# Graph layer and masked attention on one core: the last batch's output projection by head pairs, with its own copy of the weights, two queues for the last rows, and new step lists for the first and last turns

## The chip, the cores and the metric

The kernel runs on one core of one Trainium2 chip. The metric is the device time in microseconds (us): the median of the runs shown is 2990.31 us (2990.01 to 2992.61, three runs). All durations below come from one profiled execution of the kernel before, which took 2989.65 us. Its span, from the first to the last recorded event, is 2987.9 us, so 1.75 us lie around it.

## What is computed

There are 64 batches of 256 tokens with 512 features, all in fp32. For each batch the reference does two layers:

```python
deg = sum(adj, -1); agg = (adj @ x) / max(deg, EPS)
x = layernorm(x + relu(concat([x, agg]) @ W.T))          # layer 0
q, k, v = x @ Wq.T + bq, x @ Wk.T + bk, x @ Wv.T + bv     # 8 heads of 64
s = (q @ k.T) * SCALE * (adj + adj)                        # per head
x = layernorm(x + softmax(s) @ v @ Wo.T + bo)              # layer 1
```

## The kernel before, in words

All matrix products run on TensorE (PE in the profile) in fp32. One product of 128 rows by 512 columns is one instruction in the code and shows as two in the trace; the trace's "x4" is therefore two instructions.

**Steps.** The work of a batch is cut into some 215 named steps, each a few instructions on one engine (or a group of transfers). A step's name and its batch are listed by hand in three strings: START (the batches up to the first full turn, absolute batch numbers), PLAN (one turn of two batches, repeated) and END (counted back from the last batch: `:1` is batch 63, `:2` is batch 62). The engines take their instructions in exactly this order, each engine in order for itself; semaphores put in by the framework make an instruction wait for what it reads or overwrites. So the lists decide, on each of the five queues (PE, VectorE = DVE, ScalarE = ACT, GpSimd = POOL, SyncE = SP), what stands behind a waiting instruction.

**The steps that matter here.**
- `Dzx`, `Dza`, `Dadj`, `Dx`: loads of a batch's x and adj, most as four transfers each, issued by SP. `W0h0`, `W0h1`, `Wq`, `Wv`, `Wo`, `Wb`: loads of the weights and biases (Wo is one transfer of 1024 KB, Wv four of 256 KB). The built program gives the transfers eight semaphores in turn, so an issue waits until the transfer eight places before it has landed.
- `xT0`, `xT1`, `aT`, `x1T` (L401, L772, DVE): 32-by-32 transposes. `xS` (L436), `Ls` (L573), `aS`, `bS`, `yS`, `cS` (POOL): sums for the products, which are done by the Winograd form of Strassen's scheme: seven products P, L, Y, Q, V or O (numbers 1 to 7) in place of eight, gathered in three accumulators a, b, c. `W0s`, `Wqs` (L266, DVE), `Wvs`, `Wos` (POOL) and `W0i1` to `W0i7` (L291, DVE) make the weight sums, once.
- P (L582, batches 0 and 1) and L (L550, later pairs): x times W, with one and two levels of the scheme. Y (L704): adj times that. Names with k and j are the copies and additions out of PSUM: `Yk1` must have read accumulator a before `Y6` adds to it, and so on.
- `AYr`, `AYb`, `AYp`, `AYn`: residual and layer norm of layer 0. `Dway` writes its rows to DRAM, `Dz1` reads them back turned, `x1T` transposes them; Q and V follow.
- `bv1`, `bv2` (L351, 8 products with Wo), `bv3`: fold the bias of v into that of the output.
- `Sa` to `Sd` (L812): scores of head pairs a to d. `m` (L828, DVE) multiplies by adj and takes the maximum, `M` (POOL) its negative, `e` and `f` (L847, ACT) the exponentials, `r` (DVE) the reciprocal, `n` (L871, ACT) the division. `T`, `Dw`, `Ds` transpose by DVE and by way of DRAM; in the last batch `X` (L900, PE) and `XC` (copies, L907 on ACT and L909 on DVE) do it instead. `C0a`, `C0b`, `C1a`, `C1b` (L929): context of head pairs a, b, c, d, into two PSUM banks, `pc0` and `pc1`.
- `c0`, `c1` (L945, ACT) copy the context to SBUF as `cT`; `cS` sums and the O products (L497) give the output projection; `Ok`, `Oj` (L653, L478, DVE) add it to `rest`, the rows of layer 0 (`Drest`) with the bias added (`bo`, L786, POOL). `lb`, `lp`, `ln` (L660, L666 to L668, L672) are the last layer norm, per half of the tokens; `Dout` (L968) stores the rows by four transfers, all on SP.
- The PSUM pool has eight buffers of one bank, taken in turn; every S takes two. The staging buffer of `Dzx`, `Dza` and `Dz1` has two places, taken in turn.

Of the kernel before, what the change touches and what calls it, by code (L numbers as in the profile page):

```python
# [10 lines left out]
ALU = mybir.AluOpType  # L11
# [13 lines left out]
    Dzx:1 W0h0:0 Dzx:0 W0h1:0 xT1:1 xT0:1 W0s1:0 P1:1 Dza:0 xT1:0 xT0:0 Wv:0 xS3:0 P1:0 xS1:1 xS3:1 P5:1  # L25
    W0i1:0 xS1:0 Dadj:0 P5:0 xS2:1 aT:0 W0s2:0 P2:0 Pk5:0 xS2:0 Dza:1 Pk1:0 W0s4:0 Pk5:1 Pk1:1 Wvs1:0
    P6:0 W0s3:0 Dadj:1 P6:1 xS4:0 Wvs2:0 deg:0 Dx:0 P3:0 Pk6:1 Pj2:0 aS3:0 Pk6:0 Wvs4:0 P7:0 Pj3:0 Wb:0
    aS1:0 bS1:0 Y1:0 Pj7:0 Y5:0 Yk1:0 bS2:0 P4:0 Dzx:2 deg:1 aS2:0 bS3:0 Yk5:0 Y6:0 Pk4:0 Wq:0 Yk6:0
    aS4:0 bS4:0 Y7:0 xS4:1 Y3:0 Yj7:0 Y2:0 Y4:0 P3:1 Yk4:0 AYr1:0 Yj2:0 Yj3:0 P2:1 AYb1:0 AYr0:0 AYp1:0
    P7:1 aT:1 AYb0:0 AYn1:0 aS1:1 Pj7:1 AYp0:0 Dzx:3 Pj2:1 P4:1 Pj3:1 AYn0:0 xT0:2 bS1:1 bv1:0 Dway:0  # L30
    Pk4:1 Wo:0 xT1:2 Y1:1 Y5:1 Yk1:1 xS1:2 WqS:0 Y2:1 aS2:1 Yk5:1 aS3:1 bS2:1 bS3:1 Y6:1 Wqs1:0 aS4:1
    Dz1:0 Y3:1 xT1:3 xT0:3 Yk6:1 Dx:1 xS1:3 W0i5:0 bv2:0 Ls11:2 bS4:1 Wqs2:0 Ls53:2 L11:2 Ls51:2 Y7:1
    Ls12:2 Le11:2 bv3:0 L51:2 Ls52:2 L15:2 Wos1:0 Le51:2 Yj7:1 L55:2 Yj3:1 L52:2 x1T:0 Y4:1 L56:2 L16:2
    Yk4:1 yS1:0 V1:0 Yj2:1 Le16:2 Le56:2 Ls13:2 Q5:0 Ls14:2 AYr1:1 AYb1:1 Q1:0 Qk5:0 AYr0:1 AYp1:1
    AYb0:1 V5:0 W0i2:0 Qk1:0 AYp0:1 L12:2 L57:2 yS2:0 Wqs3:0 AYn0:1 L17:2 yS3:0 Vk1:0 Q6:0 AYn1:1 Wvs3:0
    Le55:2 Dway:1 Le15:2 Dadj:2 Le17:2 V6:0 Le57:2 Wqs4:0 L54:2 Vk6:0 yS4:0 L14:2 Ls54:2 V7:0 Le12:2
    Le14:2 Wos2:0 Le54:2 W0i6:0 Vk5:0 L13:2 Dza:2 Qk6:0 L53:2 Ls23:2 L21:2 Le13:2 Ls21:2 Q2:0 Le52:2
    xS2:2 Le53:2 Dx:2 Le21:2 xS2:3 W0i3:0 Q7:0 Ls63:2 Ls22:2 Ls61:2 Vj7:0 xS3:2 W0i4:0 Drest:0 L61:2
    Ls62:2 V4:0 Ls24:2 Qj2:0 xS3:3 Dz1:1 L25:2 Vk4:0 Q3:0 W0i7:0 Wos4:0 Le61:2 L26:2 Le25:2 L65:2 Le26:2
    V3:0 Qj3:0 aT:2 L27:2 L66:2 Vj3:0 bo:0 Dzx:5 L22:2 Le66:2 V2:0 Qj7:0 L62:2 L23:2 Le62:2 L67:2 Le27:2  # L40
    Ls64:2 Q4:0 Le23:2 Ls71:2 Le65:2 Le67:2 Le22:2 L24:2 Qk4:0 x1T:1 L64:2 L63:2 xS4:2 Le24:2 Sb:0 aS1:2
    Le64:2 Vj2:0 yS1:1 Sc:0 Le63:2 mb:0 xS4:3 Sa:0 Ls33:2 Ls31:2 Sd:0 mc:0 Mb:0 La12:3 fb:0 L75:2 L71:2
    ma:0 L72:2 eb:0 Mc:0 La12:2 Q1:1 ec:0 deg:2 Ma:0 Ls72:2 ea:0 L35:2 Ls74:2 Le75:2 Q5:1 Ls32:2 md:0
    Qk1:1 Ls34:2 fc:0 Le71:2 L31:2 Md:0 Dadj:3 aS3:2 V5:1 Ls73:2 ed:0 rc:0 Le35:2 yS3:1 L76:2 L32:2
    Le76:2 fd:0 yS2:1 L73:2 Dza:3 Le32:2 V1:1 rb:0 Le73:2 nc:0 rd:0 L77:2 Q6:1 Le77:2 Ls41:2 Le31:2
    Ls42:2 fa:0 Le72:2 Tc:0 La22:2 L41:2 Qk6:1 L33:2 L36:2 Dwc:0 Qk5:1 L74:2 Le36:2 Q7:1 ra:0 Le74:2
    Le33:2 Vk1:1 La22:3 na:0 Le41:2 L45:2 Qj7:1 Ls43:2 L46:2 bS1:2 Vk5:1 Le45:2 V6:1 nd:0 Ta:0 Ls44:2
    Q4:1 yS4:1 Dwa:0 Wos3:0 nb:0 Td:0 Dsc:0 L42:2 L37:2 Qk4:1 L43:2 Tb:0 V3:1 Vk6:1 Y5:2 Vj3:1 Dwb:0
    V7:1 Le46:2 bS2:2 Dwd:0 Y1:2 bS3:2 L47:2 Dsa:0 Yk1:2 aS2:2 Q3:1 Vj7:1 Le47:2 Yk5:2 Le42:2 Le43:2
    L44:2 Qj3:1 Y6:2 Dsb:0 xT1:5 Y2:2 bS4:2 Q2:1 Le44:2 aS4:2 Yj2:2 Yk6:2 xT0:5 Dsd:0 Y7:2 Le37:2 Y3:2  # L50
    Yj7:2 L34:2 Qj2:1 Y4:2 xS1:5 Yj3:2 V4:1 Le34:2 bS1:3 Yk4:2 AYr1:2 Vk4:1 Sc:1 Dzx:4 AYr0:2 Sa:1
    AYb1:2 C0a:0 AYb0:2 AYp1:2 C0b:0 ma:1 C1a:0 AYp0:2 AYn1:2 C1b:0 c0:0 mc:1 Ma:1 AYn0:2 Sd:1 c1:0
    Dway:2 aT:3 Mc:1 fa:1 Sb:1 md:1 aS1:3 ec:1 Y1:3 cS1:0 Y5:3 O2:0 deg:3 bS2:3 O1:0 bS3:3 xT1:4 aS2:3
    O5:0 xT0:4 Md:1 Ok1:0 ed:1 Y2:3 xS1:4 Yk1:3 V2:1 mb:1 Dz1:2 cS2:0 ea:1 Y6:3 cS3:0 O6:0 Yk6:3 aS3:3
    aS4:3 L51:4 Dx:3 Ok6:0 cS4:0 Y7:3 Yk5:3 Le51:4 O7:0 fd:1 Ok5:0 Mb:1 Yj7:3 bS4:3 Yj2:3 O3:0 fc:1
    Ls51:4 Oj7:0 Vj2:1 Ls13:4 Y3:3 Ls11:4 eb:1 Y4:3 rc:1 Yj3:3 Ls52:4 O4:0 rd:1 Yk4:3 Ls53:4 nc:1 L15:4
    x1T:2 L56:4 L11:4 Oj2:0 L12:4 yS1:2 Le11:4 Oj3:0 Q1:2 nd:1 Ok4:0 Ls12:4 ra:1 Tc:1 xS3:5 Ls54:4 fb:1
    V5:2 Td:1 yS3:2 Dwc:1 Dza:4 Q5:2 Vk5:2 Qk1:2 AYr0:3 AYr1:3 na:1 L55:4 rb:1 yS2:2 lb0:0 V1:2 AYb1:3
    Q6:2 Vk1:2 Qk5:2 AYb0:3 AYp1:3 Dsc:1 Ta:1 Le56:4 L52:4 Qk6:2 AYp0:3 V6:2 L16:4 Vk6:2 Ls14:4 Dadj:4
    Q7:2 nb:1 lp0:0 yS4:2 AYn0:3 L57:4 Qj7:2 V7:2 Le16:4 Tb:1 AYn1:3 Dwa:1 L17:4 Le55:4 V3:2 Le15:4  # L60
# [12 lines left out]
    Dadj:5 Yk1:4 eb:2 aS2:4 Yk5:4 Ls44:4 Le42:4 Le34:4 Ok4:1 Q1:3 yS2:3 rb:2 lb0:1 nb:2 Dsc:2 lb1:1
    lp0:1 V1:3 Le46:4 Qk1:3 Tb:2 lp1:1 L43:4 Dsd:2 L47:4 ln0:1 Y6:4 Ta:2 Vk1:3 Q6:3 aS4:4 Yk6:4 Le47:4
    Y7:4 Qk6:3 L44:4 Dwa:2 Yj7:4 V6:3 Le43:4 Dwb:2 ln1:1 xT0:6 bS4:4 Y2:4 Vk6:3 Dout:1 Y3:4 yS4:3 Qk5:3
    Y4:4 Yj3:4 Q7:3 deg:5 bS1:5 Vk5:3 xT0:7 Yj2:4 V7:3 AYr0:4 Dsa:2 V3:3 Yk4:4 Le44:4 Q3:3 xT1:7 AYb0:4
    Dsb:2 Vj7:3 Q2:3 xT1:6 Qj7:3 xS1:6 Qj3:3 xS1:7 V4:3 AYr1:4 AYp0:4 Drest:2 Q4:3 Vj3:3 AYb1:4 Dza:5
    Ls11:6 AYn0:4 AYp1:4 Sa:3 bS3:5 AYn1:4 C0a:2 xS3:7 Qk4:3 Dway:4 C1a:2 ma:3 C0b:2 Dza:6 C1b:2 Qj2:3
    c0:2 bo:2 Vk4:3 Sc:3 aT:5 Sb:3 mc:3 Sd:3 Ma:3 Ls12:6 fa:3 Dz1:4 aS1:5 mb:3 Y1:5 c1:2 ea:3 Y5:5 cS1:2
    md:3 V2:3 Dx:5 Mb:3 aS2:5 Y2:5 bS2:5 Yk1:5 O5:2 Md:3 Mc:3 ed:3 O1:2 cS2:2 Y6:5 cS3:2 fd:3 Ok1:2 O2:2  # L80
    Yk6:5 Ls51:6 ra:3 Ok5:2 eb:3 aS3:5 O6:2 Yj2:5 Ls53:6 rd:3 Yk5:5 aS4:5 na:3 L11:6 Vj2:3 cS4:2 Y7:5
    x1T:4 L51:6 bS4:5 Y3:5 fb:3 O3:2 Yj7:5 yS1:4 Ok6:2 Y4:5 nd:3 Yj3:5 O7:2 Oj3:2 Yk4:5 rb:3 Oj2:2 L15:6
    AYr1:5 Le51:6 Q5:4 ec:3 Oj7:2 AYb1:5 Le11:6 nb:3 O4:2 AYr0:5 AYp1:5 AYb0:5 V5:4 yS3:4 fc:3 Q1:4
    Ls52:6 yS2:4 rc:3 Ok4:2 lb1:2 Ls13:6 L56:6 Qk1:4 Ls14:6 Td:3 V1:4 Ls54:6 AYp0:5 nc:3 L16:6 Ta:3
# [74 lines left out]
def kernel(  # L159
# [631 lines left out]
    def last(b):  # L791
        return b == B - 1
# [234 lines left out]
```

## Time and profile before

| what | value |
|---|---|
| median of three runs | 2990.31 us |
| profiled execution / its span | 2989.65 / 2987.9 us |
| PE busy | 2946.9 us, 99% of the span |
| DVE, POOL, ACT busy | 2255.2, 1868.5, 1650.5 us |
| PE busy in 0 to 100 us | 8.80 + 18.26 + 12.57 + 19.88 + 15.44 us in five stretches of 20 |
| PE busy in 180 to 2940 us | all of it, in every stretch looked at |
| PE busy in 2940 to 2987.9 us | 18.96 of 20, 13.18 of 20, 0 of 8 |

Read PE's busy share by stretches, since its mean says nothing: it has idle time only in the first hundred microseconds and in the last fifty. In the timelines used below, a row has the start, the length, the engine, the line, the operation, output and inputs, the count, and in brackets how long the engine was idle before it and what released it. In the tables by stretch, a row has the stretch, its length, the busy time and number of instructions of PE, PE's weight loads, DVE, ACT and POOL, then PE's granted clock (1.00 is full speed), the share of the transfer engines and GB/s.

### The profile page before, as it was taken

The page shows a single profiled execution, that of the slowest core. Times are in us where ns is not written, and L with a number is a line of the kernel's source. Part 1 is how long each engine was busy: PE and PEld are TensorE (multiplying, and loading weights), DVE is VectorE, ACT ScalarE, POOL GpSimd, SP SyncE. Part 2 cuts the span into 40 slices and gives each one's busy share as a digit, 9 for nine tenths or more (in the row PEclk, how much of TensorE's full clock was granted, in tenths as well). Part 3 has the DMA queues.
Part 4 walks back from the last instruction along what each step waited for, and adds up shares of the span by engine and source line. Part 5 has one row for each costly group of instructions (what it writes and reads, how often), then busy time and mean ns, then how long its engine had stood idle before and what let it go on. Part 6 is the DMA issues. An engine that isn't in the chain of part 4 may idle for free.

```text
span 2987.9 us, 60252 instructions
## 1 busy us (share of the span) xinstructions
PE 2946.9 (99%) x18886; PEld 2578.8 (86%) x18886; DVE 2255.2 (75%) x6307; ACT 1650.5 (55%) x4999; POOL 1868.5 (63%) x3439
## 2 busy tenths in 40 slices
PE   7999999999999999999999999999999999999997
PEld 4888888888888888888888888888888888888886
DVE  6877777777777777777777777777777777777774
ACT  2455565565564555655655645556556556455565
POOL 5666566666566575666665665756666656657653
PEclk9999999999999999999999999999999999999999
DMA  7466666766657667567666577665676665775663
GB/s 168 125 186 167 178 164 158 199 175 164 179 154 190 181 168 178 164 159 197 176 164 179 154 190 183 166 178 164 158 196 175 167 180 153 190 188 162 174 173 99
DMA packets 491404, 509.71 MB, mean 171 GB/s; under 512 B 113616, under 2 KB 390096, under 8 KB 491088
## 3 DMA queue, kind: packets, MB, share of 16 engines
q1 hardware_dynamic: 490768, 505.35, 64.7%
q8 instruction: 153, 2.51, 0.4%
q14 instruction: 163, 1.34, 0.2%
q10 hardware_dynamic: 320, 0.52, 0.1%
HBM read 306.45 MB, written 199.23 MB: 169 GB/s over the span
## 4 chain that ended last, share of the span: by engine, by line
PE 96%; DMA 2%; DVE 1%; issue 1%; POOL 1%; ACT 0%; SPq 0%; ACTq 0%; POOLq 0%; DVEq 0%
PE Qa L615 15%; PE pc L929 8%; PE Qc L615 8%; PE Oa L497 7%; PE Va L497 7%; PE Qb L615 4%; PE Oc L497 4%; PE Ya L704 4%; PE Vc L497 4%; PE Ycb L704 3%; PE scc L812 2%; PE sca L812 2%; PE scb L812 2%; PE Vb L497 2%; PE scd L812 2%; PE L6a L550 2%
## 5 line engine op out<-in xcount | busy, mean ns | idle before, releaser
L631 ACT ACTIVATE qk<-Qa,bqk 128x128 f32<-128x128 f32 x768 | 219.1, 370 | 300.2 <-PE Qa L615 300.1
L666 POOL TENSOR_SCALAR mv<-mv 128x1 f32<-128x1 f32 x256 | 68.3, 267 | 369.6 <-DVE mv L661 230.5
L615 PEld LDWEIGHTS Qa<-x1T,Wq 128*128 128x128 f32 x2048 | 248.5, 192 | 6.7 <-issue 0.3
L615 PE MATMUL Qa<-x1T,Wq 128*128 128x128 f32 x2048 | 249.4, 275 | 0.0
L945 ACT COPY cT<-pc 128x512 f32<-128x512 f32 x128 | 71.9, 586 | 254.2 <-PE pc L929 254.2
L672 ACT ACTIVATE rest<-rest,mv 128x512 f32<-128x512 f32 x128 | 100.8, 809 | 169.7 <-POOL mv L668 169.6
L828 DVE CUSTOM_DVE_ANT_0 sc<-scc,adj 128x256 f32<-128x256 f32 x256 | 92.5, 418 | 113.8 <-PE scc L812 109.3
L847 ACT ACTIVATE sc<-sc,nmaxc 128x256 f32<-128x256 f32 x256 | 127.5, 500 | 76.0 <-DMA zx<-in_x_dram 34.5
L672 ACT ACTIVATE x<-oy,mv 128x512 f32<-128x512 f32 x128 | 105.2, 824 | 115.2 <-POOL mv L668 112.0
L786 POOL TENSOR_TENSOR rest<-rest,bo_sb 128x512 f32<-128x512 f32 x128 | 161.0, 1279 | 0.2 <-issue 0.2
L667 POOL TENSOR_TENSOR mv<-mv,neg_half 128x1 f32<-128x1 f32 x256 | 145.9, 570 | 21.3
L847 ACT ACTIVATE sa<-sa,nmaxa 128x256 f32<-128x256 f32 x256 | 127.0, 497 | 54.8 <-POOL nmaxa L841 52.7
L436 POOL TENSOR_TENSOR xS<-xT,xS 128x256 f32<-128x256 f32 x64 | 46.5, 728 | 175.9 <-PE L6a L550 175.9
L871 ACT ACTIVATE sb<-sb,totalb 128x256 f32<-128x256 f32 x252 | 107.5, 500 | 79.6 <-DVE totalb L859 79.6
L847 ACT ACTIVATE sb<-sb,nmaxb 128x256 f32<-128x256 f32 x256 | 127.8, 503 | 40.3 <-POOL nmaxb L841 40.3
L828 DVE CUSTOM_DVE_ANT_0 sa<-sca,adj 128x256 f32<-128x256 f32 x256 | 93.2, 420 | 73.7 <-PE sca L812 66.2
L573 POOL TENSOR_TENSOR xs<-xS 128x128 f32<-128x128 f32 x248 | 112.4, 459 | 55.2 <-PE L5cb L550 37.9
L401 DVE STREAM_TRANSPOSE xT<-zx 128x512 f32<-128x512 f32 x128 | 89.3, 700 | 66.8 <-issue 56.1
L847 ACT ACTIVATE sd<-sd,nmaxd 128x256 f32<-128x256 f32 x256 | 126.8, 497 | 18.9 <-POOL nmaxd L841 18.9
L726 DVE SCALAR_TENSOR_TENSOR oy<-Ya,deg,oy 128x256 f32<-128x256 f32 x256 | 120.5, 471 | 20.0 <-PE Ya L704 16.7
L497 PE MATMUL Oa<-Wo,cT 128*128 128x256 f32 x512 | 131.7, 380 | 1.1 <-DVE totalb L859 0.6
L497 PE MATMUL Va<-Wv,x1T 128*128 128x256 f32 x512 | 131.5, 379 | 0.0
(325 smaller groups left out, 9798.4 us busy)
## 6 DMA issues: line engine op xcount, KB each, us to landing
zx<-in_x_dram SPq DMA_DIRECT2D x256, 128.0 KB, 4.4
x<-in_x_dram SPq DMA_DIRECT2D x256, 128.0 KB, 3.8
way<-x SPq DMA_DIRECT2D x64, 512.0 KB, 2.8
z<-way SPq DMA_DIRECT2D x256, 128.0 KB, 3.2
rest<-way SPq DMA_DIRECT2D x64, 512.0 KB, 4.5
out_dram<-rest SPq DMA_DIRECT2D x256, 128.0 KB, 2.5
wsc<-sc SPq DMA_DIRECT2D x63, 512.0 KB, 3.2
wsa<-sa SPq DMA_DIRECT2D x63, 512.0 KB, 4.1
```

The lines of the kernel that those rows point to most:

```text
L497: nc.tensor.matmul(ps[:, :width].rearrange("p (m o) -> p m o", o=G), lhsT=left(k, b, c), rhs=w(OUTER[k])[:, :, c], start=first and c == 0, ...
L615: nc.tensor.matmul(ps.rearrange("p (m j q) -> p m j q", m=2, j=2)[:, m, j], lhsT=wqk(OUTER[k])[:, m, c, j * P : (j + 1) * P], rhs=left_y(k ...
L631: nc.scalar.activation(part_q(b, t, n)[:, m, j], ps.rearrange("p (m j q) -> p m j q", m=2, j=2)[:, m, j], AF.Identity, bias=bqk[:, m, c : ...
L667: nc.gpsimd.tensor_tensor(mv[:, 1:2], mv[:, 1:2], neg_half, ALU.pow)
L672: nc.scalar.activation(dst, src, AF.Identity, bias=mv[:, 0:1], scale=mv[:, 1:2])
L704: nc.tensor.matmul(ps[:, G:] if acc == "b" else ps[:, :G], lhsT=left(b), rhs=right(b), start=k in (5, 1), stop=True, skip_group_check=True,)
L726: nc.vector.scalar_tensor_tensor(h, ps[:, G:] if acc == "b" else ps[:, :G], held["deg", b][:, t : t + 1], h, ALU.mult, ALU.add)
L786: nc.gpsimd.tensor_tensor(rest, rest, bo_sb, ALU.add)
L812: nc.tensor.matmul(sc(b, j)[:, t], lhsT=qk[d, 0, hp, t * P : (t + 1) * P], rhs=qk[d, 1, hp].rearrange("d (t b m) -> d b t m", t=NT, m=L), ...
L828: nc.vector.tensor_tensor_reduce(out=s[:, :, :, r], in0=sc(b, j)[:, t].rearrange("p (a c l) -> p a c l", a=A, l=L), in1=held["adj", b][:, ...
L847: nc.scalar.activation(rows(b)[:, r], rows(b)[:, r], AF.Exp, bias=of("nmax", b)[:, r : r + 1], accum_out=of("total", b)[:, r : r + 1],)
L929: nc.tensor.matmul(ps[j * D : (j + 1) * D, hp % 2], lhsT=held["v", b][:, c, h * D : (h + 1) * D], rhs=held[f"s{name}", b][:, :, c, j * NT ...
```

## The change

- START holds the same 1110 steps in another order, PLAN is unchanged, END has 542 steps for 547. On the queues, START now issues `Wo` after `Dza:0` (before: `Wv`), `Wv` after `Dway:0` (before: `Wo`), and loads batch 0 ahead of batch 1; `bv2` moves ahead of the last P product of batch 1; the `W0i` groups stand in the order 1, 5, 4, 3, 2, 6, 7 with 5 and 4 ahead of the Y products of batches 0 and 1 (before 1, 5, 2, 6, 3, 4, 7).
- END's last batch loses the two context copies, four `cS` sums, seven O products and their seven additions. It gets: `Wo2`, a second load of Wo's 1024 KB into the buffer of `oy` of odd batches; four copies `cca` to `ccd` of 128x256 each; eight plain products U (two halves of the tokens by four head pairs, each 128x512, pairs in the order c, then a, b, d); two additions `Uk0`, `Uk1` of 128x512.
- In the last batch the softmax goes by head pairs a, c, d, b (before c, b, a, d), the context by a, c, d, b (before c, a, b, d), and `V4` stands behind the first scores.
- The last `Dout` issues two of its four transfers from ACT.

```diff
 START = """
-    Dzx:1 W0h0:0 Dzx:0 W0h1:0 xT1:1 xT0:1 W0s1:0 P1:1 Dza:0 xT1:0 xT0:0 Wv:0 xS3:0 P1:0 xS1:1 xS3:1 P5:1
...
+    Dzx:0 W0h0:0 Dzx:1 W0h1:0 xT1:0 xT0:0 xS3:0 xS1:0 W0s1:0 P1:0 Dza:0 xT1:1 P5:0 xT0:1 xS1:1 Wo:0
+    Pk5:0 P5:1 P1:1 Pk5:1 xS2:1 Pk1:0 xS2:0 Dadj:1 W0s2:0 P2:0 W0i1:0 Dzx:2 P6:0 aT:0 W0s3:0 Pk6:0 xS4:0
+    Dadj:0 Pk1:1 aS1:0 W0s4:0 P7:0 Pj2:0 Dx:0 P3:0 Pj7:0 Y1:0 Pj3:0 Wb:0 P4:0 W0i5:0 bS1:0 bS3:0 Y5:0
+    Pk4:0 xT0:2 aS3:0 P6:1 Dza:1 aS2:0 deg:0 xS3:1 Yk5:0 bS2:0 Yk1:0 Pk6:1 Wq:0 Y6:0 Y2:0 Yk6:0 aS4:0
...
 END = """
...
-    ed:1 Dout:2 C1a:1 fd:1 Xb1:1 rd:1 XCa1:1 nd:1 XCa0:1 Xd0:1 Xd1:1 XCd0:1 XCd1:1 C0a:1 XCb1:1 Drest:1
-    C0b:1 C1b:1 c1:1 c0:1 cS1:1 cS3:1 O5:1 O1:1 bo:1 O2:1 cS2:1 Ok1:1 Oj2:1 O6:1 Ok6:1 cS4:1 Ok5:1 O7:1
-    O3:1 Oj7:1 O4:1 Oj3:1 lb0:1 Ok4:1 lp0:1 lb1:1 lp1:1 ln0:1 ln1:1 Dout:1
+    XCa0:1 rb:1 XCa1:1 nb:1 Xb0:1 Xd0:1 Xb1:1 XCd0:1 Xc0:1 XCb1:1 XCb0:1 C0a:1 XCc0:1 Drest:1 C1a:1
+    C1b:1 C0b:1 ccc:1 ccd:1 cca:1 U20:1 ccb:1 U21:1 U01:1 U10:1 bo:1 U30:1 U00:1 U11:1 Uk0:1 U31:1 lb0:1
+    Uk1:1 lp0:1 lb1:1 ln0:1 lp1:1 ln1:1 Dout:1
 """
...
+    @step("Wo2")
+    def _(b):
+        wo_last = tile_of("wo_last", b, [P, FC, F], tag="oy1")
+        nc.sync.dma_start(out=wo_last, in_=wot.rearrange("(c p) o -> p c o", p=P))
+
+    def last_output(hp, name):
+        @step(f"cc{name}")
+        def _(b):
+            ctx_T = part_of("cT", b, [P, FC, NT, P])[:, hp].rearrange("p t q -> p (t q)")
+            nc.scalar.copy(ctx_T, held[f"pc{hp // 2}", b].rearrange("p (n q) -> p n q", n=2)[:, hp % 2])
+
+        def product(t):
+            @step(f"U{hp}{t}")
+            def _(b):
+                ps = bank(f"U{t}", b) if hp == 2 else held[f"U{t}", b]
+                nc.tensor.matmul(
+                    ps,
+                    lhsT=held["cT", b][:, hp, t],
+                    rhs=held["wo_last", b][:, hp],
+                    start=hp == 2,
+                    stop=True,
+                    skip_group_check=True,
+                )
+
+        for t in range(NT):
+            product(t)
+
+    for hp, name in enumerate("abcd"):
+        last_output(hp, name)
+
+    def add_output(t):
+        @step(f"Uk{t}")
+        def _(b):
+            rest = held["rest", b][:, t]
+            nc.vector.tensor_tensor(rest, held[f"U{t}", b], rest, ALU.add)
...
     @step("Dout")
     def _(b):
         for a, part in groups():
-            nc.sync.dma_start(out=token_rows(out[b], a), in_=held["rest", b][part])
+            queue = nc.scalar if last(b) and a % 2 else nc.sync
+            queue.dma_start(out=token_rows(out[b], a), in_=held["rest", b][part])
```

## The prediction

> **What bounds the kernel now.** First the chain of work that ended last, by engine:
>
> ```profile
> PE 96%; DMA 2%; DVE 1%; issue 1%; POOL 1%; ACT 0%; SPq 0%; ACTq 0%; POOLq 0%; DVEq 0%
> ```
>
> PE is the bound, so only two things can change the time: PE's work, and the places where PE stands idle. The work hardly changes, so I looked for the idle time, by stretches:
>
> ```profile
> 0.00:20.00 20.00, 8.80 (x17) 3.40 (x18) 7.20 (x11) 1.28 (x1) 4.42 (x10) 1.00 1.03 191
> ...
> 40.00:60.00 20.00, 12.57 (x36) 7.71 (x35) 12.55 (x22) 4.12 (x5) 13.63 (x21) 0.74 0.93 211
> ...
> 80.00:100.00 20.00, 15.44 (x74) 12.66 (x74) 16.23 (x30) 1.51 (x5) 10.48 (x14) 0.83 0.40 88
> ...
> 2960.00:2980.00 20.00, 13.18 (x72) 8.17 (x68) 6.32 (x15) 6.53 (x17) 5.69 (x8) 1.00 0.18 52
> ```
>
> Idle time stands at the two ends alone, where the lists are new; the clock is also below 1 there (0.74, 0.83), so "busy" hides a loss. PE's timeline shows the waits:
>
> ```profile
> 47.50 0.70 PE L704 MATMUL Ya<-yB,aS 128*128 128x256 f32 x2 [1.98 <-POOL yB L573]
> 49.61 1.22 PE L704 MATMUL Ycb<-oy,aS 128*128 128x256 f32 x2 [1.41 <-POOL aS L436]
> 54.08 5.84 PE L351 MATMUL p_bv<-Wo,bv_all 128*128 128x256 f32 x16 [3.25 <-DMA Wo<-in_wot_dram]
> ...
> 90.21 1.22 PE L550 MATMUL L2a<-W,xs 128*128 128x256 f32 x2 [3.32 <-DVE oy L563]
> ...
> 2963.55 1.96 PE L900 MATMUL Xd<-ident,snd 128*128 128x128 f32 x8 [1.84 <-ACT snd L871]
> ...
> 2970.46 1.13 PE L497 MATMUL Oc<-Wo_sums,cS 128*128 128x256 f32 x4 [1.98 <-POOL cS L436]
> ```
>
> `bv2` waits for Wo and then takes 5.84 us, where eight products of 128x256 at 0.43 (a Y's spacing) are 3.44. L21 waits for `W0i2` behind DVE's other work. The same stretches finer:
>
> ```profile
> 48.00:49.00 1.00, 0.20 (x1) 0.00 (x0) 0.56 (x1) 0.00 (x0) 1.00 (x1) 0.58 1.11 344
> ...
> 88.00:89.00 1.00, 0.00 (x0) 0.00 (x0) 1.00 (x2) 0.00 (x0) 0.88 (x2) 1.00 0.00 0
> 89.00:90.00 1.00, 0.00 (x0) 0.00 (x0) 1.00 (x4) 0.00 (x0) 0.00 (x0) 0.56 0.00 0
> ...
> 96.00:97.00 1.00, 1.00 (x8) 0.92 (x7) 1.00 (x4) 0.00 (x0) 0.53 (x2) 1.00 0.00 0
> ```
>
> The clock halves some 2.5 us after PE goes idle (idle from 86.9, halved at 89.4) and comes back after 4.1 us (54.1 to 58.2) and 5.7 us (90.2 to 95.9) of work. A stall of 3.3 us so costs 3.3 plus half of that: 2.0 to 2.9. The gap of 1.84 at 2963 cost no clock.
>
> **START, step by step.** Spacings read off the timelines: P 1.72, Y and L 0.43, Q 1.78, V 0.86; on DVE Yk 0.40, P additions 0.60, xT 0.62, deg 1.0, stats 0.85, W0i 1.5 alone (67.0 to 68.5) and 2.6 beside POOL (51.3 to 53.9); POOL sums 0.42 and 0.70. I let each engine take the new list, each instruction when its engine is free and its inputs are there. Landings go by bytes ahead of them, as before.
>
> - To 10.9 us nothing changes: 1 MB of W and one batch's x must land, batch 0's now in batch 1's place. First P to 14.4 at half clock, as before.
> - The P products: `W0h1` lands at 18.0, W0s2 ends at 19.3, W0i1 and aT come ahead of W0s3 (22.7). P7:0 directly behind P6:0 waits for the copy `Pk6` (0.58 + issue): 0.65 idle. P6:1 ends at 31.5. Y6:0 then waits for Yk1:0 at 32.6, since W0i5, xT0:2 and deg now stand ahead of it on DVE: 1.1 idle. Y4:0 ends at 35.5 (before 36.0).
> - P7:1, P2:1, P3:1 to 40.7; **bv2** now at full clock with Wo landed at about 24.5 (Wv's old place in the queue), 3.44, to 44.1; P4:1 to 45.9. Before, P4:1 ended at 44.0, without bv2.
> - Y:1: W0i4 on DVE ahead of Yk1:1 and zx3's landing ahead of Yk5:1 leave PE 1.05 and 1.25 idle, Yj7:1 behind two Wqs 0.7. With Y and ten L, PE is done at 56.2.
> - x1T:0 needs z1:0. The bytes queued ahead are the same sum as before (Wv in Wo's place), and AYn1:0 ends at 41.9 for 43.4, so way goes 1.5 us earlier, but all transfers up to x1 were through at 57.8 before and the queue was full; I take z1:0 landed at 56, x1T done at 57.2, Q1:0 at 58.0. Before, V1:0 started at 63.64 with three L fewer done (1.3 us): **6.9 us gained** so far.
> - From Q1:0 to the first score: 18 L, 7 Q, 6 V are 7.8 + 12.5 + 5.2 = 25.5. DVE has four W0i left here for five. L21 waits for W0i2 (69.7): 0.85, L26 for Le21: 0.6. Scores at 85.0. Before, 99.76 less V2:0 (0.86), which now comes later: 98.9.
>
> So 13.9 gained without a clock loss. The idle places at 47 to 50 are 2.3 us within 2.75; before, 3.4 within 3.9 halved the clock (48.4). By that nearest row, half of such a spell is at stake, and a spell costs 2.0 to 2.9. I charge 1.5 and take the scores at 86.5: **12.4 us**. Both ends: 13.9, and 5 if z1:0 lands 3 us later and two spells of 2.9 come.
>
> [...]
>
> What hides the rest: after the scores PE had no idle time to 2940 before, and DVE, busy 15.9 to 18.8 of 20 us there, has the same work. The softmax of batch 0 returned at 135.5 for a context at 135.3 before; now scores at 86.5, the last T about 100, return by 110, and C1a at about 120: 10 us to spare.
>
> **END, step by step**, from the end q of the last Q4 (2940.2 before). V4 (0.86) moves behind the scores, so q comes 0.86 earlier. The first score waits for Qk4 (1.0), the first `m` for the context of batch 62 that still reads the same tile, so the first exponential starts at q+4.9 (before q+5.0). ACT then has, in order: sixteen exponentials (0.49 each, 7.84), sixteen divisions (0.40 each, 6.4), c1, V, c0 (1.3), two ln (1.55), XCa0 (0.5): 17.6. Md stands behind bo:2 (2.5) on POOL: 0.8 idle; small waits 0.5. The last division (b) ends at q+23.8; before it ended at q+24.5. But then X of b, d, b, c (4 x 0.43) and four contexts (4 x 0.9) follow, for one X and three contexts before: last context at q+29.1, before q+28.3.
>
> PE meanwhile has nothing from q+19.7 (Xc1) to q+23.8: 4.1 us idle, longer than the 2.5 that halved the clock at 89.4. The X and contexts then run at half clock for some 4 to 5.7 us: 2.0 to 2.9 more. I take 2.7: q+31.8.
>
> After the last context: before, cT copy, cS, O and additions to the end of ln1 took 2982.92 - 2968.43 = 14.5. Now the copies (0.35 each) are hidden under C1b and C0b but the last, which U10 needs 1.7 us later; eight U of 0.86 (P's 1.72 is two such) end 6.95 after; Uk1 0.7, stats 0.9, POOL 1.2, ln1 0.8 with waits 0.2: 10.75. **3.75 us gained.** Dout by two queues: four issues took 1.74 from 2982.95; two beside two: 0.87 gained, nothing if the landing is set by the bytes. Drest lands by q+30, bo by q+33, Uk0 at q+37: hidden.
>
> Wo2, 1024 KB, is issued about 2921, where the transfer engines stood idle before (2918 to 2922, 2924 to 2926.7), and costs them 5 us; Dsb:2, the last of batch 62, landed about 2944.5 for C0b:2 at 2946.1. Slack 1.4 us; bounds 0 and 3 (c0:2 stands ahead of five divisions and exponentials on ACT, so late is late one for one). I take 0.
>
> Sum of END: -0.86 + 0.8 + 2.7 - 3.75 - 0.87 = **-2.0**; without the clock loss -4.7, with it and 3 us from Wo2 +1.
>
> **Sum:** 12.4 + 2.0 = 14.4 off 2989.65 is 2975.25; the median stood 0.66 above the profiled execution, so **2975.9**.
>
> **Rivals.**
> - *START gives half:* PE's gaps go but z1:0 lands 3 us later behind Wv's four transfers and the clock drops twice, or DVE, with W0i5 and W0i4 ahead, holds the Yk. For: DVE was the releaser at 90.21. Gain 5 + 2: 2983.3.
> - *No clock loss anywhere:* 13.9 + 4.7: 2971.7. For: the gap at 2963 cost none. Against: 2.5 us did at 89.4.
> - *What START gives, END takes back:* Wo2 holds an eighth of the lanes until it lands, 9.3 us in the loaded queue like Wo at 44.8, and Dsc:2 or Dsb:2 behind it. Gain within 6 us: 2987.
> - *Slower:* the same lane, if Dsb:2 comes so late that c0:2 shifts ACT's whole chain: 9.3 + 5 of bytes - 1.4 = 13, END +11. From the point where START gives less than 11 minus 6, slower by over 6: 2997. Against: the idle stretch at 2918.
>
> **Chances.** 0.2% is 6 us, about what a measurement of this kernel can tell from no change. Forecast (2973 to 2980) 0.55; no clock loss 0.12; START half 0.20, of which 0.03 within 6 us; END takes back 0.07; slower 0.06. Faster 0.84, same 0.10, slower 0.06. The range leaves out the last two and a little of the best case: 2969.5 to 2986.5.
>
> **What would show it.** p_bv without a wait and near 3.6 us; first score at 85 to 88; the clock at 0.5 for some us at the last X; ln1 some 10.8 us after the last context; two out transfers on ACT. Wrong if PE shows idle time between 100 and 2930 us, or if x1T:0 starts after 60.

## The result, and the profile after

| | us |
|---|---|
| kernel after, median of 9 runs | 2981.73 (2980.28 to 2983.38) |
| kernel before, beside it, 9 runs | 2989.78 (2987.36 to 2992.61) |
| ratio | 0.9975 [0.9964, 0.9985] |
| profiled execution after / its span | 2980.28 / 2978.4 (before 2989.65 / 2987.9) |

The change is worth 8.05 us; 14.4 were forecast. The direction is as forecast, the size is not: 2981.73 lies inside the prediction's whole range (2969.5 to 2986.5), but outside its forecast's own (2973 to 2980), and nearer to the rival "START gives half" (2983.3) than to the forecast (2975.9).

The chain of work that ended last, by engine, now has its DMA share gone:

```profile
PE 98%; POOL 1%; DVE 0%; DMA 0%; issue 0%; ACT 0%; ACTq 0%; POOLq 0%; DVEq 0%
```

In PE's timeline of START, `bv2` waits for nothing and takes 3.62 us (before 3.25 of waiting and 5.84). The waits of more than 0.8 us that are left between the first product and the first score are all for DVE; another of 0.67 stands ahead of Y4:0 at 38.0:

```profile
34.97 0.67 PE L704 MATMUL Ya<-yB,aS 128*128 128x256 f32 x2 [2.20 <-DVE oy L726]
...
43.69 3.62 PE L351 MATMUL p_bv<-Wo,bv_all 128*128 128x256 f32 x16
...
51.83 0.67 PE L704 MATMUL Ya<-yB,aS 128*128 128x256 f32 x2 [1.42 <-DVE oy L726]
53.40 0.69 PE L704 MATMUL Ycb<-oy,aS 128*128 128x256 f32 x2 [0.91 <-DVE oy L726]
...
90.60 1.13 PE L812 MATMUL scd<-qk 64*128 64x256 f32 x8
```

And of END:

```profile
2950.70 0.60 PE L900 MATMUL Xc<-ident,snc 128*128 128x128 f32 x4
2954.36 1.67 PE L900 MATMUL Xb<-ident,snb 128*128 128x128 f32 x4 [3.06 <-ACT snb L871]
...
2962.17 7.13 PE L959 MATMUL U<-wo_last,cT 128*128 128x512 f32 x16
```

Four products of X are 0.60 at full clock (the row at 2950.70); the three groups behind the wait take 1.06 each. Between the two ends nothing moved: from the first score to the first score of batch 63 it was 2841.43 us before (99.76 to 2941.19) and 2841.55 after (90.60 to 2932.15); V2:0 came into this stretch and V4 went out of it, 0.86 each. So the two profiled spans differ by 9.16 at the first score (8.30 of it START's, 0.86 being V2:0), minus 0.12 in the middle, plus 0.40 from batch 63's first score to the end (1.26 END's, V4 being in it now): together 9.4, the difference of the two spans (2987.9 and 2978.4, each rounded).

### The profile page after: what moved, and what is told of

Read it like the earlier page. It is cut to its first block, busy times and chain, and to the rows that moved or that the text cites. A ratio compares the mean times of both kernels' runs of the same rounds, so it can differ in the third digit from the quotient of the medians.

```text
span 2978.4 us, 60255 instructions
## 1 busy us (share of the span) xinstructions
PE 2946.3 (99%) x18874; PEld 2575.6 (86%) x18874; DVE 2252.4 (76%) x6302; ACT 1651.1 (55%) x5001; POOL 1862.6 (63%) x3435
## 4 chain that ended last, share of the span: by engine, by line
PE 98%; POOL 1%; DVE 0%; DMA 0%; issue 0%; ACT 0%; ACTq 0%; POOLq 0%; DVEq 0%
PE Qa L615 15%; PE pc L929 8%; PE Qc L615 8%; PE Va L497 7%; PE Oa L497 7%; PE Qb L615 4%; PE Vc L497 4%; PE Oc L497 4%; PE Ya L704 4%; PE Ycb L704 3%; PE sca L812 2%; PE scc L812 2%; PE scd L812 2%; PE scb L812 2%; PE Vb L497 2%; PE Ob L497 2%
```

## The experiments

All times are medians, each with its ratio to the kernel before in runs on the same chip. The kernel before had medians of 2989.85, 2990.05 and 2990.11 beside the three groups of kernels (e1 to e4, e5 to e8, e9 to e12). Where a kernel is compared with the kernel after, that is across groups, with the 2981.73 above. "First score" is the start of the first L812 product in the profile.

**e1_start_only.** The kernel before with the new START.

```diff
-START = """  (before's list)
+START = """  (after's list)
```

> The kernel before with the new START list alone; END, the output projection and the last store as before. Theory (START gives most): the first score product starts at 90.6 us as in the changed kernel (before 99.8), and the time is 7 to 8.5 us under that of before. Rival (the gain is END's, START's is given back in the turns between): 2 us or less under before, although the first score is early. The stretch from the first score to the last Q product of batch 63 should be 2840.4 us as before if nothing is given back, and 2841.5 if it is what the changed kernel's profile shows.

Measured: 2986.23 (2982.62 to 2986.87), ratio 0.9986 [0.9977, 0.9995]: 3.6 us. The profiled run took 2983.17, first score 92.22. The runs lie in two groups, 2982.6 to 2984.1 and 2986.2 to 2986.9. Neither the theory's 7 to 8.5 us nor the rival's 2 came. From the first score to that of batch 63 it took 2842.34 us, with V2:0 and V4 both in this stretch; less 0.86 for each that is 2840.6, the same as before's 2841.43 less V4. So the turns between give nothing back.

**e2_end_only.** The kernel after with the old START.

```diff
-START = """  (after's list)
+START = """  (before's list)
```

> The changed kernel with the START list of before: only END's order, the plain output projection with its second load, and the two queues. Theory: 2 to 3 us under before, the sum read off the profile after (V4 behind the scores 0.9, the clock halved at the last transposes against it, 3.5 after the last context, nothing from the two queues). Rival (END is the main gain): 6 us or more under before.

Measured: 2986.56 (2985.61 to 2989.35), ratio 0.9992 [0.9983, 1.0001]: 3.3 us less than before (the interval just reaches 1, so no difference is not quite excluded), and 4.8 more than the kernel after. From the last Q of the last batch to the end of the span it took 49.23 us, against 49.63, 49.56 and 49.63 in the three profiles with the old END (before, e1, e9) and 48.13 in the kernel after. So by the profiles END is worth 0.4 to 1.5, while by the runs START is worth 3.6 to 4.8 and END the rest.

What was not expected: its START is before's, instruction for instruction, and its first score is at 95.72, not 99.76. The same wait for VectorE stands in it, equally long (before's row stands in the prediction, at 90.21):

```profile
88.99 0.70 PE L550 MATMUL L2a<-W,xs 128*128 128x256 f32 x2 [3.33 <-DVE oy L563]
```

but this product takes 0.70 and before's took 1.22: the clock did not fall here. That made the clock the thing to look at.

**The clock's grid.** In the tables by stretch I dated every fall and return of the granted clock from the stretches that hold them (a stretch of 1 us at a mean of 0.67 holds 0.66 us at half). The spells of half clock last 3.42 us (after, 53.92 to 57.34), 6.82 (e1, 34.56 to 41.38), 10.24 (before, 48.16 to 58.40): one, two, three times 3.413 (a third of 10.24). The falls of one run are whole multiples of it apart: 35.38 and 55.86 in e3 (6.0), 48.16 and 89.12 in before (12.0), 53.92 and 2955.26 in after (850.0). So in these profiles the clock changed at the edges of windows of 3.413 us that ran on through the whole execution, and where START's waits lay in the windows differed from run to run (the wait at 86.9 starts 1.2 us behind an edge in before; in e2 the same wait has an edge inside it, at 87.19). Cut by these windows, PE's busy time (third column) against the clock (third from the right), before, around the wait at 86.9 to 90.2:

```profile
85.71:89.12 3.41, 1.18 (x6) 0.70 (x4) 3.38 (x5) 0.00 (x0) 3.17 (x3) 1.00 0.01 1
89.12:92.53 3.41, 2.32 (x6) 1.88 (x7) 2.83 (x9) 0.00 (x0) 0.00 (x0) 0.50 0.02 5
```

in e2, where the same wait falls across an edge:

```profile
83.77:87.18 3.41, 1.89 (x10) 1.34 (x8) 3.38 (x3) 0.00 (x0) 3.41 (x4) 1.00 0.04 10
87.19:90.60 3.41, 1.61 (x7) 1.44 (x8) 3.41 (x10) 0.00 (x0) 0.47 (x1) 1.00 0.00 0
```

in the kernel after, whose wait of 2.20 ahead of Y6:0 (32.77 to 34.97) is cut at 33.44, and whose waits of 1.42 and 0.91 lie in one window:

```profile
33.44:36.85 3.41, 1.72 (x7) 1.24 (x8) 2.05 (x6) 0.00 (x0) 1.29 (x3) 1.00 1.03 209
50.51:53.92 3.41, 1.19 (x5) 0.79 (x6) 3.41 (x8) 1.04 (x1) 2.70 (x6) 1.00 1.14 195
53.92:57.33 3.41, 3.41 (x10) 2.66 (x9) 3.38 (x4) 0.37 (x1) 3.33 (x3) 0.50 1.13 215
```

and in e1, where the wait ahead of Y6:0 (2.21) lies in one window:

```profile
31.15:34.56 3.41, 1.20 (x5) 0.55 (x4) 2.50 (x6) 0.58 (x1) 1.47 (x3) 1.00 0.95 201
34.56:37.97 3.41, 2.76 (x7) 1.39 (x6) 1.91 (x5) 0.00 (x0) 2.03 (x3) 0.50 1.06 220
```

The first rise fits the grid too. The first P product takes 3.75 us in the kernel after, later ones 1.88; the clock column reads 1.00 there, so that this is half clock is inferred from the two lengths. In the kernel after an edge lies at 53.92 less eleven windows, 16.38, inside the two P products behind the first; in e1 one lies at 34.56 less six windows, 14.08, ahead of them. The row of these two, after and then e1:

```profile
14.33 4.62 PE L582 MATMUL Pc<-W_sums,xS 128*128 128x512 f32 x8
```

```profile
14.33 3.60 PE L582 MATMUL Pc<-W_sums,xS 128*128 128x512 f32 x8
```

Over START, behind the first P products, in the ten profiles in which the clock fell there (all but e7, e9, e11 and e12): every window at full clock with 2.09 us or more of idle time was followed by half clock (12 of 12); with 1.57 to 1.98 three were (before 1.98, e4 1.73, e10 1.57) and three were not (e8 1.97, e2 1.80, after 1.69); with 1.52 or less, none. Half clock lasted until a window had at most 0.46 idle; one with 0.65 (e1 at 34.56, the wait ahead of Y4:0) kept it for another. By the half of 3.41, an estimate, each such window costs up to 1.7 us where PE is the bound; e5 measures 1.4 for one. At END, too, every window with 2.2 us or more of idle time was followed by half clock, in the nine profiles that have tables by 1 us there (all but e4, e7, e8, e11 and e12; in the kernel after 2.65 us idle from 2951.85, half clock from 2955.26). The same START list has its first score at 99.76 in before's profile and at 95.72 in e2's, with five and two windows of half clock; only one run of each kernel is profiled, so how much of the spread of the runs is the grid is not shown.

**e3_one_queue.** The kernel after, the last rows by one queue.

```diff
-            queue = nc.scalar if last(b) and a % 2 else nc.sync
-            queue.dma_start(out=token_rows(out[b], a), in_=held["rest", b][part])
+            nc.sync.dma_start(out=token_rows(out[b], a), in_=held["rest", b][part])
```

> The changed kernel with all four last stores on SP. Theory (what ends the run is the landing of the last rows, and ACT's transfers land later: 3.2 us against 2.2): from the end of the last ACTIVATE to the end of the span 4.9 to 5.2 us, as with two queues, and the same time within 0.3 us. Rival (the four issues of 0.43 us in a row set the end, as the prediction put it): 0.9 us more from the last ACTIVATE to the end, 6.0 us.

Measured: 2981.79 (2979.98 to 2982.79), ratio 0.9971 [0.9961, 0.9982]: not to be told from the kernel after. Its START fell the worse way (first score 92.77 for 90.60), so the ends are to be compared. From the end of the last ln1 (2973.22; here 2975.32) to the end of the span it took 5.18 us with two queues and 4.78 with one. In all fourteen profiles it is 5.1 to 5.5 in the seven with two queues and 4.7 to 5.0 in the seven with one. The issue, first with two queues, then with one:

```profile
2973.25 0.98 SPq L1009 DMA_DIRECT2D out_dram<-rest  x2
2973.26 0.86 ACTq L1009 DMA_DIRECT2D out_dram<-rest  x2
```

```profile
2975.35 2.14 SPq L1008 DMA_DIRECT2D out_dram<-rest  x4
```

The issue is shorter by 1.2, as counted, and the end is not earlier: the landing sets it (the four rows of the kernel after landed 2.0 to 3.4 us after their issue, 3.2 in the median). By the profiles the second queue costs 0.4 rather than gaining 0.87; the medians of the runs do not tell the two apart.

**e4_w0i_later.** The kernel after, three of VectorE's steps moved down in START.

```diff
-  ... Wb:0 P4:0 W0i5:0 bS1:0 ... AYn1:0 aT:1 Dway:0 aS1:1 P4:1 bv3:0 bS1:1 ... Pk4:1 W0i4:0 Y1:1 ... Yk6:1 Dx:1
+  ... Wb:0 P4:0 bS1:0 ... AYn1:0 aT:1 W0i5:0 Dway:0 aS1:1 P4:1 bS1:1 ... Pk4:1 Y1:1 ... Yk6:1 bv3:0 Dx:1
-  ... W0i7:0 L22:2 ...
+  ... W0i7:0 W0i4:0 L22:2 ...
```

> The changed kernel with three DVE groups moved in START: W0i5 from ahead of Yk1 of batch 0 to behind aT of batch 1, W0i4 from ahead of Yk1 of batch 1 to behind W0i7, bv3 behind Yk6 of batch 1. Theory (in the new START PE waits for DVE additions that stand behind weight sums, and these waits drop the clock at 53.9 us): the waits of 2.20, 0.67, 1.42 and 0.91 us before Y products go for the most part, the clock stays at 1 between 50 and 60 us, the first score is at 84.5 to 86.5 and the time 4 to 6 us under the changed kernel. Rival (the landing of the rows for batches 2 and 3 and of the turned rows sets the stage): the first score moves by 1 us or less.

Measured: 2979.32 (2979.21 to 2979.48), ratio 0.9966 [0.9952, 0.9979], 2.4 less than the kernel after. DVE's rows of the kernel after, the last sum of W0i5 (which began at 29.19) and the addition Yk1:0 that Y6:0 waits for, and then Yk1:0 in e4:

```profile
31.25 0.67 DVE L291 TENSOR_TENSOR W_inner<-W_sums,W_inner 128x256 f32<-128x256 f32 x1
...
34.35 0.47 DVE L726 SCALAR_TENSOR_TENSOR oy<-Ya,deg,oy 128x256 f32<-128x256 f32 x1
```

```profile
32.76 0.48 DVE L726 SCALAR_TENSOR_TENSOR oy<-Ya,deg,oy 128x256 f32<-128x256 f32 x1
```

Without W0i5 it comes 1.6 us earlier (0.4 of that is P's, which ended earlier too), Y6:0 waits 0.98 for 2.20, and P4:1 ends at 47.3 for 48.9. But then POOL is late: its sums of 128x128, 0.45 us each at 51, take 1.3 and 1.4 at 53 to 57 while DVE does the Wq sums (in the kernel after, too, such sums take 1.44 at 53.8 and 1.32 at 57.0 beside them), and L55 and L56 wait for them, 1.36 and 1.11; the first:

```profile
54.73 0.70 PE L550 MATMUL L5cb<-W_inner,xs 128*128 128x256 f32 x2 [1.36 <-POOL xs L573]
```

The clock fell at 56.48 for two windows; the first score came at 89.85 only. So W0i5 did hold the Yk; what was to be had behind it was given to the next late engine.

**e5_keep_clock.** The kernel after, with six idle products of 128x256 on constant weights ahead of Xb0 of the last batch, into the bank that Xb0 overwrites.

```diff
-  ... nb:1 Xb0:1 Xd0:1 ...
+  ... nb:1 k6X:1 Xb0:1 Xd0:1 ...
```

> The kernel after, with six products of 128x256 on constant weights ahead of Xb0 of the last batch, where TensorE waits 3.06 us; they write the bank that Xb0 then overwrites, so the result is not touched. Theory: the X and contexts ran at 0.5 to 0.67 of the clock because of that wait; with six products of 0.43 (2.6 us) in it the clock stays at 1, and from the last division of pair b to the end of the last context takes 5.6 us in place of 7.8: 2979.5 us, 2.2 less than the kernel after's 2981.73. Rival: the contexts wait for the copies of X on ScalarE and VectorE in any case, the clock only fills their waits, and the time stays at 2981.7.

Measured: 2980.43 (2978.91 to 2981.49), ratio 0.9966 [0.9952, 0.9979]; 1.3 less than the kernel after, the intervals of the two overlap. In the profile:

```profile
2953.32 2.75 PE L1017 MATMUL Xb<-W 128*128 128x256 f32 x12
2956.54 1.52 PE L900 MATMUL Xb<-ident,snb 128*128 128x128 f32 x4 [0.46 <-ACT snb L871]
```

The X behind Xb0 are back at 0.60 and the clock stays at 1.00. From Xb0 to the first U (2962.91) it took 6.37 us, and 7.81 in the kernel after: the clock loss is there and is 1.4 us, one window.

**e6_winograd_tail.** The kernel after, with the old output projection behind the new contexts, without `Wo2`.

```diff
-  ... C1b:1 C0b:1 ccc:1 ccd:1 cca:1 U20:1 ccb:1 U21:1 U01:1 U10:1 bo:1 U30:1 U00:1 U11:1 Uk0:1 U31:1 lb0:1 Uk1:1 ...
+  ... C1b:1 C0b:1 c1:1 c0:1 cS1:1 cS3:1 O5:1 O1:1 bo:1 O2:1 cS2:1 Ok1:1 Oj2:1 O6:1 ... O3:1 Oj7:1 O4:1 Oj3:1 lb0:1 Ok4:1 ...
```

> The kernel after, with the output projection of the last batch as before (two copies of the context, cS, seven O with Ok and Oj) behind the same contexts, and no second load of Wo. Theory: the plain projection ends 11.05 us behind the last context and the old one 14.5, so this one is 3.4 us slower than the kernel after: 2985.1. Rival: the plain projection gains nothing of its own and END's gain lies in the order of the pairs: 2981.7, or below it if the 1024 KB of Wo2 hold another transfer.

Measured: 2984.96 (2983.44 to 2986.46), ratio 0.9983 [0.9974, 0.9992], 3.2 more than the kernel after. Behind the last context PE waits for POOL's cS again, 1.49 and 1.07 us. From the end of the last context (2963.78) to the end of ln1 (2977.82) 14.04 us; in the kernel after 11.05 (2962.17 to 2973.22). The plain projection alone is worth 3.0, and its second load of Wo costs nothing that shows: the middle takes 2841.55 us with it and without.

**e7_start_warm.** e4 with nine idle products in START's idle places, into banks of their own.

```diff
-  ... Y6:0 ... Y4:0 ... Y3:1 ... L55:2 ... L56:2 ...
+  ... k2Y:0 Y6:0 ... k1Y:0 Y4:0 ... k1Y:1 Y3:1 ... k3Y:1 L55:2 ... k2Y:1 L56:2 ...
```

> The kernel of e4, with 9 products of 128x256 on constant weights in five of START's idle places (two ahead of Y6:0, one ahead of Y4:0, one ahead of Y3:1, three ahead of L55:2, two ahead of L56:2), into banks of their own. They compute nothing that is read. Theory: the clock's fall at 57 in e4 came from 3.5 us of idle time in five pieces since 49; filled, it stays at 1 from 15 us on, the first score comes at 87 to 88 in place of 89.85, the time is 2977 and the spread of its runs under 1 us. Rival: the next thing that is late (x1T:0 at 58 to 59, POOL's sums) holds Q1:0 as it did, and the time stays at 2979.3.

Measured: 2978.44 (2977.12 to 2979.26), ratio 0.9960 [0.9947, 0.9972]. From the second P product to 108 us the clock stayed at 1.00, Q1:0 starts at 58.80 (e4 61.65) and the first score comes at 87.36. The median is only 0.9 below e4's, and the spread (2.1) is not smaller, against what I expected; e4's five runs lie so close together (0.3) that they may all have had one grid.

**e8_old_warm.** The kernel before with 21 idle products.

```diff
-  ... Y6:1 ... Y3:1 bv2:0 ... L24:2 ...
+  ... k4Y:1 Y6:1 ... k3Y:1 Y3:1 k7Y:1 bv2:0 ... k7S:0 L24:2 ...
```

> The kernel before, START and END as they were, with 21 products of 128x256 on constant weights in START's four idle places (four ahead of Y6:1, three ahead of Y3:1, seven ahead of bv2, seven ahead of L24:2). They compute nothing that is read. Theory: in before's profile the clock was halved over two stretches of work, 54.1 to 58.2 and 90.2 to 95.9, worth 2.0 and 2.9; with it kept at 1 the first score comes at 94 to 95 in place of 99.76 with the same waits, the time is 2985 and the runs lie within 1 us of each other. Then of START's change only 5 to 6 us are the list itself, and the rest of what the prediction counted was clock. Rival: the waits end when the transfers and VectorE end, the time is theirs, and it stays at 2989.8 with the old spread.

Measured: 2992.19 (2989.66 to 2997.44), ratio 1.0010 [1.0001, 1.0018]: slower. The seven last ones stood ahead of the wrong step: the product that waits 3.3 us is L27:2, for the addition Le26:2, which stands behind the four sums of W0i7 on VectorE (84.87 to 89.16 in before's profile); the 3.0 us of idle products came on top. And 2.09 of the wait for Wo were left; the clock fell behind it. Its eleven runs spread over 7.8 us, more than before's; the reason is not known. The kernel tells nothing on the question; e9 puts the products in the right places.

**e9_old_warm2.** As e8, with four more ahead of bv2 and the last seven ahead of L27:2.

```diff
-  ... Y6:1 ... Y3:1 bv2:0 ... L27:2 ...
+  ... k4Y:1 Y6:1 ... k3Y:1 Y3:1 k7Y:1 k4Y:1 bv2:0 ... k7Y:1 L27:2 ...
```

> The kernel before with 25 products of 128x256 on constant weights in START: as in e8, but four more ahead of bv2 (where TensorE still waited 2.09 us for Wo in e8 and the clock fell at 55), and the last seven ahead of L27:2, which is the product that waits 3.3 us for Le26:2; in e8 they stood ahead of L24:2, where nothing waits, and cost their 3.0 us. Theory: with the clock at 1 throughout, the first score comes at 95 to 96 (99.76 in before's profile), the time is first score plus 2889.9 as in before, 2985.5, and the runs lie within 2 us. That is the old list without clock losses. Rival: the waits for Wo and for VectorE set the time and take back what the clock gives: first score at 98 or later, 2988 or more.

Measured: 2986.33 (2985.69 to 2987.42), ratio 0.9987 [0.9978, 0.9996]. Nothing but idle work was added, and the kernel is 3.8 us faster than before; its eleven runs lie within 1.7 us (before, in 17 runs on the same chip: 4.6). From the second P product on the clock is 1.00 through START, and the first score:

```profile
95.31 1.13 PE L812 MATMUL scb<-qk 64*128 64x256 f32 x8
```

4.45 earlier than in before's profile, with the same transfers and the same VectorE. The span gained only 3.3, since from the first score to that of batch 63 it took 2842.58 for 2841.43: among other things a context now waits 0.9 for a transfer of `Ds` (pair b). So of the old START's 99.76, 4.45 were the clock.

**e10_new_warm.** The kernel after with eleven idle products in START.

```diff
-  ... Y6:0 ... Y4:0 ... Y6:1 Y3:1 ... L55:2 ...
+  ... k4Y:1 Y6:0 ... k1Y:1 Y4:0 ... k3Y:1 Y6:1 ... k2Y:1 Y3:1 ... k1Y:1 L55:2 ...
```

> The kernel after with 11 products of 128x256 on constant weights in START's idle places (four ahead of Y6:0, one ahead of Y4:0, three ahead of Y6:1, two ahead of Y3:1, one ahead of L55:2). They compute nothing that is read. Theory: the clock stays at 1; the first score comes at 88 to 89 (90.60, 92.22, 92.77 in the profiles of this list), the time is 2978.3. Against e9 it gives the new list's worth without the clock: 6 us, of which V2:0, moved behind the scores, is none (0.86 comes back later). Rival: VectorE's Yk and x1T hold it as before, 2981.7.

Measured: 2981.45 (2980.48 to 2981.64), ratio 0.9971 [0.9959, 0.9982]: the rival's time, 2981.7. The clock stayed at 1 past both old places, and then POOL's sums held L55 for 1.71 us, as in e4. That wait (56.3 to 58.05) lies mostly in one window, and the clock fell at its edge, 2 us after PE was at work again:

```profile
56.61:60.02 3.41, 1.84 (x6) 1.03 (x7) 3.14 (x5) 0.00 (x0) 3.34 (x6) 1.00 1.15 192
60.02:63.43 3.41, 3.41 (x10) 2.70 (x9) 3.27 (x6) 0.37 (x1) 3.33 (x3) 0.50 0.04 9
```

First score 90.92. From this I take it that in the kernel after the half clock at 54 to 57 was partly free, since PE at full speed would have stood before POOL; that is argued, not shown.

Beside e9 this first score is 4.39 earlier, 0.86 of it V2:0. So with the clock held in the old list, and in the new one but for this one window, the new list is worth 3.5 us up to the first score; the two medians, END included, are 4.9 apart, and 6 were expected.

**e11_all and e12_half_on_dve.** e11 is e7 with e5's six products and e3's one queue. e12 is e11 with two of the four divisions of pair b of the last batch on VectorE, and four products for six.

```diff
-                nc.scalar.activation(dst, src, AF.Identity, scale=of("total", b)[:, r : r + 1])
+                if last(b) and name == "b" and r >= 2:
+                    nc.vector.tensor_scalar(dst, src, of("total", b)[:, r : r + 1], None, ALU.mult)
+                else:
+                    nc.scalar.activation(dst, src, AF.Identity, scale=of("total", b)[:, r : r + 1])
```

> The kernel of e7 (W0i5, W0i4 and bv3 later on VectorE, nine products in START's idle places) with the six products of e5 ahead of Xb0 of the last batch and all transfers of the output on SyncE's queue as in e3. Theory: the gains add: 2978.4 - 1.4 - 0.4 = 2976.7. Rival: what e5 and e3 gave lies in the spread of the runs, and the time stays at 2978.4.

> The kernel of e11 with two of the four divisions of pair b of the last batch on VectorE in place of ScalarE, and four products ahead of Xb0 in place of six. Theory: ScalarE's chain of exponentials and divisions sets END's beginning, Xb waits for its last row, so Xb starts 0.8 us earlier (two divisions of 0.40): 2975.9. Rival: VectorE reaches them later than ScalarE would have, or its sum of exponentials is not there sooner, and the time is that of e11 or worse.

Measured: e11 2975.97 (2975.56 to 2977.25), ratio 0.9953 [0.9941, 0.9966]; e12 2975.71 (2974.90 to 2976.45), ratio 0.9952 [0.9939, 0.9964]. e11's 2.5 below e7 is more than the 1.8 expected; from batch 63's first score to the end it took 44.38 (e7 46.36, after 46.25). e12's medians differ from e11's by less than either's spread; in the profiles this stretch is 43.77, 0.6 shorter. Xb0 was expected to start earlier; it starts 22.20 us after batch 63's first score in both. But from its start to that of the next X it takes 0.78 us (2951.63 to 2952.41) in place of e11's 1.36 (2951.82 to 2953.18): its four products read one division each, and the last divisions come sooner. So ScalarE's divisions do set the end of Xb0, but the step is too small to be told by the runs. Both beat the kernel after by some 6 us.

## Why the prediction was right in sign and wrong in size

- **START, "12.4 us": the step that failed.** In the two profiles it gave 8.3, in the runs 3.6 to 4.8, and with the clock held (e9 and e10) 3.5 up to the first score. Three parts of it were wrong.
  - *The clock.* I took it that "the clock halves some 2.5 us after PE goes idle" and that it comes back after a stretch of work, so that the two spells of before's profile belonged to its list. They belong to the list and the grid together. The fall at 48 I put down to two waits, "3.4 within 3.9"; it came at 48.16, before the second of them (1.41 us, from 48.20) had begun, and the window up to it had 1.98 us of idle time. The old list with the clock held (e9) has its first score at 95.31; the difference of 4.45 to 99.76 was counted as certain gain, but e2, with the same list, had it at 95.72. For the new list I charged 1.5; its profiles lost one window (after) or three (e1, e3, e5, e6), and their first scores are 90.60, 92.22, 92.77, 92.80 and 92.38.
  - *VectorE's order.* "Y6:0 then waits for Yk1:0 at 32.6 ... 1.1 idle": Yk1:0 ran at 34.35 and the wait was 2.20. W0i5 took 2.7 us beside POOL (29.19 to 31.9); the 1.5 of a W0i alone would have fitted my 32.6, and the row of 2.6 stood in my own list. deg took 1.35 for 1.0. The two P products behind the first took 4.62 (3.60 in e1, 3.65 before), another 1.0; that is the grid again, the clock's first rise at 16.38. P4:1 ended at 48.9 for 45.9. e4 takes 1.2 off this wait by moving W0i5. This is the rival "START gives half", by its DVE branch; its other branch, z1:0 late, did not come: x1T:0 ran at 57.9 to 59.1 and Q1:0 waited for L products, not for it.
  - *POOL.* It was no term of mine at this place; e4 and e10 show it next in line with 1.4 and 1.7 us.
  - From Q1:0 to the first score it took 28.45 for 27.0. Waits of 0.24, 0.5 and 0.8 are in it; I did not break down the rest.
- **A misreading, without effect on the sum:** I put the wait of 3.32 at 90.2 down to L21 waiting for W0i2. The rows show L27 waiting for Le26:2 behind W0i7. That cost e8.
- **END, "-2.0".** One term was booked wrongly: V4 stood behind the last Q4 before, so moving it does not bring q forward, and the -0.86 was not there; the other terms make -1.1. Measured from the last Q to the end: 1.5 less in the kernel after's profile, 0.4 in e2 and e10, where the half clock at the X lasted two windows (6.8 us) in place of one. Term by term:
  - With q at 2932.2, the first exponential came at q+4.0, not q+4.9: the first score, of pair a, does not wait for Qk4. Md's 0.8 of idle time was there (0.81). The last division ended at q+23.3 (23.8).
  - Clock loss at the last X: "2.7", measured 1.4 by e5, and 1.1 more in e2 and e10, where it lasted two windows. The wait was 3.06 us for 4.1.
  - The last context ended at q+30.0 (31.8 with the clock loss and 29.1 without).
  - The plain projection: 11.05 us behind the last context for 10.75. Its gain of 3.75 measured 3.0 by e6, since the old tail took 14.04 there in place of 14.5.
  - "Dout by two queues: 0.87 gained": wrong. It costs 0.4; the alternative I had named, that the landing sets it, fits the rows.
  - Wo2 hidden: right, at 0. No idle time of PE between 100 and 2940 us.
- **In part luck.** That the time lies inside the range owes something to the range's low end, "5 if z1:0 lands 3 us later and two spells of 2.9 come". Clock losses did come (one to three windows), but z1:0 did not hold Q1:0: the room that was left for it went to VectorE's order and to POOL. And before's profile, from which the sum starts, had five windows of half clock in START where e2, with the same list, had two.
- **What the runs leave open.** By the runs END gives 3.3 (e2 against before) to 4.5 (after against e1); by the profiles 0.4 to 1.5. Only one run of each kernel is profiled, and the grid moved START by 4.0 us between before's profile and e2's, so I hold the profiles' END for the better number; I did not settle it. Nor did I find where e1's second group of runs loses its 3 us. That the grid makes the spread of the runs fits e9, whose runs drew together, but not e7, whose did not, nor e8, whose spread grew.

## What to carry to other kernels

Before a stall of TensorE is priced, date the clock's falls and cut PE's idle time into the windows they lie on. Here the same wait of 3.3 us cost its own length in e2 and, in before, two windows of half clock besides (89.12 to 95.95); and in the kernel after two waits of 1.42 and 0.91 us in one window were followed by half clock as that one was. A baseline profile with such a spell must not be counted as the list's own time; idle products in the waits show what the list itself is worth, and can be left in where they fit. And when one engine's wait is shortened, work the next engine through with the durations it has beside the others, not alone (a W0i group took 1.5 us alone and 2.7 beside POOL).

## What the runs showed of the hardware that was not expected

- The granted clock changed on a grid of 3.413 us that ran on unbroken (850 windows between two falls of one run). In START it fell behind all 12 windows at full clock with 2.09 us or more of idle time and behind three of six with 1.57 to 1.98; 0.65 us in a window at half clock kept it there (e1).
- POOL's sums of 128x128 went from 0.45 to 1.3 and 1.4 us while VectorE made the Wq sums (e4, 53 to 57 us).
- Two queues for four transfers of 128 KB took 1.2 us off the issue and nothing off the end; the two of ACT landed 3.2 us after issue in the median, the six that SP issued in the last 27 us of the same profile 2.2.
